# The factor of a normalisation read from a PSUM column instead of SBUF, in a selective-scan layer

## The chip, the cores and the metric

The kernel runs on one core of one Trainium2 chip. The metric is the device time of the whole program in microseconds (us). Engines are called PE (TensorE), DVE or VectorE, ACT or ScalarE, POOL or GpSimd, and SP (the queue that issues most DMAs).

## The reference

Four layers follow each other, each with a residual: `x = x + layer(group_norm(x))`. Only layer 0 is touched here. It is a two-dimensional selective scan over 4 images of 64 x 64 positions and 128 channels, with an inner width of 256:

```
xz = x @ in_proj_w.T ; xh, z = split(xz) ; z = silu(z)
xc = silu(depthwise_conv3x3(xh) + conv_b)
xs = 4 scans of xc: by rows, by columns, and both reversed
h  = exp(delta * A) * h + (delta * u) * B      # along 4096 positions, 16 states per channel
y  = sum over states of h * C, + D * u ; the four directions are summed
mu = y.mean(-1) ; var = y.var(-1)              # over the 256 inner channels of one position
y  = (y - mu) / sqrt(var + EPS) * out_norm_w + out_norm_b
out = (y * z) @ out_proj_w.T
```

The inner norm, `(y - mu) / sqrt(var + EPS)`, is what the change touches. Layers 1 to 3 (a Fourier layer, a layer of spectral convolutions with attention, a neighbourhood attention) come afterwards.

## The kernel before

**The main loop of layer 0.** Work is cut into 128 units: 4 images x 4 directions x 8 chunks of 512 positions (`units`, `per` = 32 units to an image). A unit has 16 slots (`NS`), one for each state number n. A slot does the following, for both halves s of the 256 channels: POOL makes `dB` = du x B (L476, one instruction of 128 x 1024), ACT makes `dA` = exp(delta x A) into a PSUM bank (L482; three banks, pool `psx`), and DVE runs the scan `h` (L483). PE then transposes the finished `h` of an earlier slot (L370, one buffer `pt` of two banks), ACT copies the result to SBUF (L380), and PE contracts over the states (L405). The inputs of the next unit (`inputs`: xd_ps, dp, delta, du) are made in slots 6 to 13 of the current one.

**Side work.** Two generators are woven into the slots. `before` prepares the next image (group norm, in projection, convolution), `after` finishes the previous image (inner norm, gate, out projection, residual). `after` of image b runs during the units of image b + 1; that of the last image has no units left to lie beside and is run in one go at the end (`d.finish(flush_all)`), the drain. Image 0 has no `after` beside it, and the last image no `before`.

`after` works by chunks of 512 positions, held as 4 groups q of 128 positions on the partitions with the 256 channels along the free axis. Means and variances are aggregated once per image into `mv`, and `rs` = 1/sqrt(var + eps) is a tile of 128 x 32 in SBUF. For each chunk: load `y` (called yf in the profile) and `z` (zf); normalise yf in place, four DVE instructions (L256); transpose it on PE into the bank `pg` (L264); scale and shift on ACT into `yg`; multiply with zf on POOL (L270); project on PE into the bank `op` (L275); add the residual on DVE (L281) and store.

**What sets the order.** The order on PE, ACT, DVE and POOL is the one in which the program is written out (`tc.manual_schedule`). The generators stop at `yield` with the kind of step that comes next: "l" a load, "f" a free step, "m" a step that needs the PSUM bank, "z" and "c" matmuls of `before`. At the end of each slot the loop lets at most one step through that needs the bank, `before` ahead of `after`, and only where `free` holds: not in slots 6 to 10 (`BUSY`), not while a convolution is under way, and not before slot `taken`. Steps "f" and "l" go through as soon as they are due. `Side(pieces, count, first, slots)` paces a generator: `count` steps are spread over `slots` slots. `later(place, f, ...)` puts an instruction off to a following slot: "dve" ones are written ahead of that slot's scans, "act0", "act1" and "act2" between its ACT instructions. A call through it stands at line L437 in the profile.

**The bank.** `spare(name)` takes a tile from the pool `psm`, which has a single PSUM bank (tag "m"). In the loop xd_ps, dp, all PSUM tiles of `before`, and pg and op of `after` go through this one bank. The buffers of yf and zf come from a ring of four that the accumulators `y` of the units also use (tag "t4").

Of the kernel before, what the change touches and what calls it, by code (L numbers as in the profile page):

```python
# [12 lines left out]
ALU = mybir.AluOpType  # L13
# [3 lines left out]
P = 128  # L17
# [9 lines left out]
NS = 16  # L27
# [55 lines left out]
def layer0(sh, A, x_in, x_out, scr):  # L83
# [6 lines left out]
    tc, nc = sh.tc, sh.nc  # L90
    with ExitStack() as ctx:
# [144 lines left out]
        def after(b, st, later):  # L236

            mv = small.tile([P, NJ, 2], F32, name="ln_mv")
            for j in range(NJ):
                if j % 8 == 0:  # L240
                    yield "f"
                nc.vector.bn_aggr(mv[:, j, :], st[:, j])
            rs = sh.rstd(small, mv[:, :, 1], [P, NJ], "ln_r")
            exp_and_ln()
            for c in range(NCH):
                yield "l"
                rows = slice(c * CH, (c + 1) * CH)
                y = tmp.tile([P, 4, 2 * P], F32, name="yf", tag="t4", bufs=4)
                nc.sync.dma_start(y, tiles(scr(f"y2{b % 2}")[rows, :]))
                z = tmp.tile([P, 2, CH], F32, name="zf", tag="t4", bufs=4)  # L250
                nc.sync.dma_start(z, scr(f"z{b % 3}")[:, :, rows].rearrange("s p t -> p s t"))
                for q in range(4):
                    if q % 2 == 0:
                        yield "f"
                    j = 4 * c + q
                    nc.vector.tensor_scalar(  # L256
                        y[:, q, :], y[:, q, :], mv[:, j, 0:1], rs[:, j : j + 1], ALU.subtract, ALU.mult
                    )
                yg = tmp.tile([P, 2, CH], F32, name="yg", bufs=1)
                for s in range(2):  # L260
                    yield "m"
                    pt = spare("pg")
                    for q in range(4):
                        nc.tensor.transpose(pt[:, q * P : (q + 1) * P], y[:, q, s * P : (s + 1) * P], sh.ident)  # L264
                    norm = dict(scale=on_w[:, s : s + 1], bias=on_b[:, s : s + 1])
                    later("act0", nc.scalar.activation, yg[:, s, :], pt, AF.Identity, **norm)
                yield "f"
                xr = tmp.tile([P, 4, DM], F32, name="xr", tag="t2", bufs=4)
                nc.sync.dma_start(xr, tiles(x_in(b)[rows, :]))
                nc.gpsimd.tensor_tensor(yg, yg, z, ALU.mult)  # L270
                yield "m"
                op = spare("op").rearrange("p (q d) -> p q d", q=4)
                for q in range(4):
                    for s in range(2):
                        nc.tensor.matmul(  # L275
                            op[:, q, :], lhsT=yg[:, s, q * P : (q + 1) * P], rhs=w_out[:, s, :], start=(s == 0), stop=(s == 1)
                        )
                later("dve", residual, b, rows, xr, op)

        def residual(b, rows, xr, op):  # L280
            nc.vector.tensor_tensor(xr, xr, op, ALU.add)  # L281
            nc.sync.dma_start(tiles(x_out(b)[rows, :]), xr)
# [51 lines left out]
        spare = lambda name: psm.tile([P, CH], F32, name=name, tag="m")  # L334
# [94 lines left out]
        sides = []  # L429
        taken = 0  # L430
        BUSY = range(6, 11)
        todo = {}
        slot = 0

        def later(place, f, *a, slots=1, **kw):

            todo.setdefault((slot + slots, place), []).append(lambda: f(*a, **kw))  # L437

        def flush(place, at=None):
            for f in todo.pop((slot if at is None else at, place), ()):  # L440
                f()
# [6 lines left out]
        with tc.manual_schedule(engines=order):  # L448
            for i, (b, k, c) in enumerate(units):
                if i % per == 0:  # L450
                    ln_st = small.tile([P, NJ, 1, 6], F32, name="ln_st")
# [12 lines left out]
                for n in range(NS):  # L464
                    slot = NS * i + n
                    g, q = divmod(n, 4)
                    if q == 0:
                        B_now = Bb
                        if g < 3:
                            Bb = broadcast(bd, g + 1)  # L470
                        elif i + 1 < len(units):
                            Bb = broadcast(bd_next, 0)
                        h = tmp.tile([P, 2, CH, 4], F32, name="h", bufs=3)
                        G = dict(unit=unit, g=g, h=h, q=0)
                    dB = tmp.tile([P, 2, CH], F32, name="dB", bufs=3)
                    nc.gpsimd.tensor_tensor(dB, du, B_now[:, q : q + 1, :].to_broadcast([P, 2, CH]), ALU.mult)  # L476
                    flush("dve")
                    if i + 1 < len(units) and n in (9, 11):
                        next(coming)
                    for s in range(2):  # L480
                        dA = psx.tile([P, CH], F32, name="dA", tag="x")
                        nc.scalar.activation(dA, delta[:, s, :], AF.Exp, scale=A_neg[:, k, s, n : n + 1])  # L482
                        nc.vector.tensor_tensor_scan(  # L483
                            h[:, s, :, q], dA, dB[:, s, :], state[:, s, n : n + 1], ALU.mult, ALU.add
                        )
                        if s == 0 and i + 1 < len(units):
                            if n in (7, 8, 10):
                                next(coming)
                        elif n == 7 and i + 1 < len(units):
                            bd_next, Wd_next = next(coming)  # L490
                        flush(f"act{s}")
                    copy = transposed() if slot >= LAG else (lambda: None)
                    copy()
                    flush("act2")
                    if q == 2:
                        W = Ws[g] = tmp.tile([P, 32, 16], F32, name="W", bufs=4)
                        nc.sync.dma_start(W, Wd[g, 0 : P * CH].rearrange("(p t a) -> p t a", p=P, a=16))
                    if q == 3:
                        queue.append(G)
                        if c < NCH - 1:  # L500
                            later("act1", nc.scalar.copy, state[:, :, 4 * g : 4 * g + 4], h[:, :, CH - 1, :], slots=5)

                    if i + 1 < len(units):
                        if n == 1:
                            u_next, v_next = fetch(*units[i + 1])
                        if n == 6:
                            coming = inputs(*units[i + 1][1:], v_next, (i + 1) % 2)
                        if n in (6, 7, 9):
                            next(coming)
                        if n == 13:  # L510
                            ready = next(coming)

                    if n == 10:
                        y = unit["y"] = tmp.tile([P, 4, 2 * P], F32, name="y", tag="t4", bufs=4)
                        if k == 0:
                            src = scr("y3").rearrange("(w q r) d -> r w q d", w=64, r=2)
                            for r in range(2):
                                nc.sync.dma_start(y[64 * r : 64 * r + 64], src[r, :, 4 * c : 4 * c + 4, :])
                        elif k != 1:
                            nc.sync.dma_start(y, dst(1 if k == 3 else 0))  # L520

                    inside = [d for d in sides if d.inside]
                    free = n not in BUSY and not inside and slot >= taken
                    able = dict(f=False, l=False, m=free, z=free and n != 5, c=free and n == 11)
                    for d in inside or [d for d in sides if able[d.need] and d.due(slot)][:1]:
                        taken = slot + dict(m=1, z=2, c=3)[d.need]
                        d.free_at = slot + 1
                        d.step()
                    for d in sides:
                        if d.need in ("f", "l") and d.due(slot):  # L530
                            if d.need == "l":
                                d.free_at = slot + 3
                            d.step()
                    sides = [d for d in sides if d.need]
                if i + 1 < len(units):
                    u, bd, Wd = u_next, bd_next, Wd_next
                if i % per == per - 1:
                    slot += 1
                    for d in sides:
                        d.finish(flush_all)  # L540
                    sides = [Side(after(b, ln_st, later), 4 + 8 * 7, NS * (i + 1) + 8, 28 * NS)]
            while queue or copied:
                transposed()()
            for d in sides:
# [1269 lines left out]
```

## Time and profile before

| | |
|---|---|
| median of 3 runs | 8517.93 us (8517.77 to 8523.15) |
| profiled execution | 8527.0 us |
| layer 0's loop of 2048 slots | from 255 to 6143 us |
| drain of layer 0 | to about 6257 us |
| layers 1 to 3 | the rest, about 2270 us |
| busy over the span | DVE 81%, PE 78%, ACT 74%, POOL 64% |

A line of a group reads: line of the program, engine, operation, output <- inputs, shapes, count | busy us in all, mean ns of one | idle us of the engine just before them, and who ended the most of it. A line of the timeline reads: start, length, engine, line, operation, with the idle time ahead of it in brackets. Neighbouring instructions of one group are drawn together in a timeline (x2, x4).

### The profile page before, as it was taken

To read this page: it belongs to the slowest core of one execution; us is meant where nothing else is said; L and a number is where in the kernel's file an instruction comes from. 1 tells how busy PE (TensorE), PEld (TensorE's weight loads), DVE (VectorE), ACT (ScalarE), POOL (GpSimd) and SP (SyncE) were. 2 spreads that over 40 slices of the span, in tenths; PEclk is the share of its full clock that TensorE was granted. 3 is DMA by queue.
4 is the path that set the end of the run, shared out by engine and by line. 5 is a ranking of instruction groups with operands and counts; after the bars stand their busy time and mean duration, and the time that the engine had idled before them with its cause. 6 is when DMAs were issued, how large, how long until landed. Compare 5 with 4: busy or idle time off the path is not lost. (4 is left out here: it accounts for less than half of the span.)

```text
span 8527.0 us, 140477 instructions
## 1 busy us (share of the span) xinstructions
PE 6643.2 (78%) x52976; PEld 4210.6 (49%) x52976; DVE 6867.5 (81%) x7956; ACT 6352.6 (74%) x10268; POOL 5488.4 (64%) x2502
## 2 busy tenths in 40 slices
PE   7688888777788777878877777777668978586689
PEld 3344454444445444444544444444457766464456
DVE  2689999998999999899999999999835454646578
ACT  6799999988988898898888988988812222414467
POOL 0689988988888898888888899999700011020133
PEclk9799999999999999999999999999979989798799
DMA  5445555445555544455554445444341032230332
GB/s 109 137 148 167 171 169 167 167 149 153 181 158 171 169 162 154 154 167 173 169 172 162 153 145 180 166 165 171 132 112 49 23 91 68 81 102 28 91 94 79
DMA packets 1281978, 1163.78 MB, mean 136 GB/s; under 512 B 637974, under 2 KB 1075826, under 8 KB 1214355
## 3 DMA queue, kind: packets, MB, share of 16 engines
q1 hardware_dynamic: 1279618, 1153.06, 42.7%
q8 instruction: 417, 6.83, 0.3%
q14 instruction: 263, 2.15, 0.1%
q10 hardware_dynamic: 1680, 1.74, 0.1%
HBM read 962.66 MB, written 189.74 MB: 135 GB/s over the span
## 5 line engine op out<-in xcount | busy, mean ns | idle before, releaser
L476 POOL TENSOR_TENSOR dB<-du,Bb 128x1024 f32<-128x1024 f32 x2048 | 4821.2, 2385 | 677.6 <-DVE h L483 500.7
L483 DVE TENSOR_TENSOR_SCAN h<-dA,state,dB 128x512 f32<-128x512 f32 x4096 | 4957.1, 1270 | 372.7 <-ACT dA L482 274.3
L370 PE MATMUL pt<-ident,h 128*128 128x128 f32 x16384 | 2268.5, 283 | 1071.8 <-ACT hT L380 1065.6
L482 ACT ACTIVATE dA<-delta,A_neg 128x512 f32<-128x512 f32 x4096 | 2756.3, 693 | 206.3 <-DVE h L483 184.4
L370 PEld LDWEIGHTS pt<-ident,h 128*128 128x128 f32 x16384 | 1854.7, 143 | 2123.0 <-ACT hT L380 1866.6
L380 ACT COPY hT<-pt 128x1024 f32<-128x1024 f32 x2048 | 2072.1, 1012 | 192.5 <-PE pt L370 178.8
L405 PE MATMUL yT<-hT,W 128*32 128x256 f32 x16384 | 1403.1, 415 | 3.1 <-DVE y L421 2.6
L862 POOL COPY XG<-Xs 64x9 f32<-64x9 f32 (+2 forms) x44 | 10.9, 293 | 1028.9 <-DVE in_st L862 675.8
L206 PE MATMUL cv<-xn,taps 128*128 128x512 f32 x1152 | 622.9, 642 | 17.3 <-DVE e L222 8.8
L405 PEld LDWEIGHTS yT<-hT,W 128*32 128x32 f32 x16384 | 454.0, 150 | 355.9 <-issue 341.6
L1535 POOL TENSOR_TENSOR S<-S,sm 128x784 f32<-128x784 f32 x128 | 191.3, 1494 | 406.5 <-DVE sm L1533 342.2
L316 PE MATMUL dp<-xd,w_dt 65*128 65x512 f32 x512 | 299.0, 667 | 127.4 <-ACT Ct L303 91.0
L325 POOL TENSOR_TENSOR du<-delta,u 128x1024 f32<-128x1024 f32 x128 | 305.1, 2384 | 81.8 <-DVE delta L322 81.8
L206 PEld LDWEIGHTS cv<-xn,taps 128*128 128x128 f32 x1152 | 186.3, 191 | 259.2 <-issue 243.5
L297 PE MATMUL xd_ps<-u,w_x 128*48 128x512 f32 x512 | 256.9, 626 | 46.2 <-DMA u<-l_xw 19.5
L1542 ACT ACTIVATE S<-S,mx 128x196 f32<-128x196 f32 x512 | 229.1, 451 | 33.9 <-DVE mx L1569 33.4
L316 PEld LDWEIGHTS dp<-xd,w_dt 65*128 65x128 f32 x512 | 79.2, 195 | 242.4 <-ACT Ct L303 149.0
L672 ACT ACTIVATE h<-pf,b 128x512 f32<-128x512 f32 x128 | 88.2, 689 | 146.5 <-PE pf L671 146.5
L322 DVE SCALAR_TENSOR_TENSOR delta<-delta,dp 128x512 f32<-128x512 f32 x256 | 169.5, 662 | 28.4 <-ACT delta L320 28.4
L319 ACT ACTIVATE delta<-dp 128x512 f32<-128x512 f32 x256 | 152.8, 597 | 52.7 <-PE dp L316 48.7
L1411 POOL MEMSET kp<- 128x210 f32 (+1 forms) x8 | 1.8, 285 | 275.2 <-DMA x<-m 275.2
L256 DVE TENSOR_SCALAR yf<-yf,ln_mv,ln_r 128x256 f32<-128x256 f32 x128 | 169.2, 1368 | 3.2 <-DMA yf<-l_y 3.2
(334 smaller groups left out, 7444.9 us busy)
## 6 DMA issues: line engine op xcount, KB each, us to landing
Bb<-l_B SPq DMA_DIRECT2D x512, 1024.0 KB
W<-l_W SPq DMA_DIRECT2D x512, 256.0 KB
l_y<-y SPq DMA_DIRECT2D x128, 512.0 KB
u<-l_xw SPq DMA_DIRECT2D x64, 512.0 KB
y<-l_y SPq DMA_DIRECT2D x64, 512.0 KB
u<-l_xr SPq DMA_DIRECT2D x64, 512.0 KB
V<-l_v SPq DMA_DIRECT2D x512, 49.0 KB
wr<-wt SPq DMA_DIRECT2D x128, 136.0 KB
```

The source lines that it names most:

```text
L206: nc.tensor.matmul(pm, lhsT=taps[:, s, t, :], rhs=xn[:, dy : dy + 8, dx : dx + 64], start=(t == 0), stop=(t == 8),)
L297: nc.tensor.matmul(xd_ps, lhsT=w_x[:, s, k, :], rhs=u[:, s, :], start=(s == 0), stop=(s == 1))
L316: nc.tensor.matmul(dp, lhsT=w_dt[:, k, s * P : (s + 1) * P], rhs=xd, start=True, stop=True)
L325: nc.gpsimd.tensor_tensor(du, delta, u, ALU.mult)
L370: nc.tensor.transpose(pt[:, j, s, :], G["h"][:, s, t0 : t0 + 32, :].rearrange("p t n -> p (t n)"), sh.ident)
L380: return lambda: nc.scalar.copy(hT, pt.rearrange("p j s d -> p j (s d)"))
L405: nc.tensor.matmul(U["yT"][e][32 * jo : 32 * jo + 32, qo % 2, :], lhsT=U["Ws"][G["g"]][:, :, 4 * q + j], rhs=hT[:, j, :], start=((e, jo) n ...
L476: nc.gpsimd.tensor_tensor(dB, du, B_now[:, q : q + 1, :].to_broadcast([P, 2, CH]), ALU.mult)
L482: nc.scalar.activation(dA, delta[:, s, :], AF.Exp, scale=A_neg[:, k, s, n : n + 1])
L483: nc.vector.tensor_tensor_scan(h[:, s, :, q], dA, dB[:, s, :], state[:, s, n : n + 1], ALU.mult, ALU.add)
L1535: nc.gpsimd.tensor_tensor(Sv, Sv, U["sm"].unsqueeze(2).to_broadcast([P, 4, 196]), ALU.mult)
L1542: nc.scalar.activation(Sn, Sn, AF.Exp, bias=U["mx"][:, n : n + 1], accum_out=sm[:, n : n + 1])
```

## The change

The four normalising instructions of a chunk become `scalar_tensor_tensor`: the mean is still a per-partition scalar from SBUF, but the factor is now a second tensor operand, a PSUM column spread over the 256 elements with a stride of zero. ACT copies the chunk's four columns of `rs` into the bank first (`nb`). The chunk's two "f" steps become one step "n" that needs the bank, may not fall into slot 5, and keeps it for two slots; its four instructions are put off to the following slot with `later`. The number of steps of `after` is given as 52 instead of 60.

```diff
                 z = tmp.tile([P, 2, CH], F32, name="zf", tag="t4", bufs=4)
                 nc.sync.dma_start(z, scr(f"z{b % 3}")[:, :, rows].rearrange("s p t -> p s t"))
+                yield "n"
+
+                nb = spare("nb")[:, 0:4]
+                nc.scalar.copy(nb, rs[:, 4 * c : 4 * c + 4])
                 for q in range(4):
-                    if q % 2 == 0:
-                        yield "f"
-                    j = 4 * c + q
-                    nc.vector.tensor_scalar(
-                        y[:, q, :], y[:, q, :], mv[:, j, 0:1], rs[:, j : j + 1], ALU.subtract, ALU.mult
-                    )
+                    later("dve", normed, y[:, q, :], mv[:, 4 * c + q, 0:1], nb[:, q : q + 1])
...
+        def normed(y, mean, factor):
+            nc.vector.scalar_tensor_tensor(y, y, mean, factor.to_broadcast([P, 2 * P]), ALU.subtract, ALU.mult)
...
-                    able = dict(f=False, l=False, m=free, z=free and n != 5, c=free and n == 11)
+                    able = dict(f=False, l=False, m=free, n=free and n != 5, z=free and n != 5, c=free and n == 11)
                     for d in inside or [d for d in sides if able[d.need] and d.due(slot)][:1]:
-                        taken = slot + dict(m=1, z=2, c=3)[d.need]
+                        taken = slot + dict(m=1, n=2, z=2, c=3)[d.need]
...
-                    sides = [Side(after(b, ln_st, later), 4 + 8 * 7, NS * (i + 1) + 8, 28 * NS)]
+                    sides = [Side(after(b, ln_st, later), 4 + 8 * 6, NS * (i + 1) + 8, 28 * NS)]
```

## The prediction

> **What bounds the kernel now.** I read the page's table of groups first, then the stage by stage table of busy time cut at the starts of the four images of layer 0, then the groups of VectorE alone in the stretch where the changed line runs, then its waits, and last the timeline around single instructions of the line and in the drain after the last scan.
>
> The groups of the page show the loop of layer 0 and the line that is changed:
>
> ```profile
> L476 POOL TENSOR_TENSOR dB<-du,Bb 128x1024 f32<-128x1024 f32 x2048 | 4821.2, 2385 | 677.6 <-DVE h L483 500.7
> L483 DVE TENSOR_TENSOR_SCAN h<-dA,state,dB 128x512 f32<-128x512 f32 x4096 | 4957.1, 1270 | 372.7 <-ACT dA L482 274.3
> L482 ACT ACTIVATE dA<-delta,A_neg 128x512 f32<-128x512 f32 x4096 | 2756.3, 693 | 206.3 <-DVE h L483 184.4
> L256 DVE TENSOR_SCALAR yf<-yf,ln_mv,ln_r 128x256 f32<-128x256 f32 x128 | 169.2, 1368 | 3.2 <-DMA yf<-l_y 3.2
> ```
>
> To see there: POOL's longest idle time is ended by VectorE's scan, and VectorE's own idle time is only 373 us over the whole loop. The changed line takes 1368 ns for 256 elements, though a scan over 512 takes 1270.
>
> The table by image (stretches of 512 slots each; columns are the length, then PE, weight load, DVE, ACT, POOL busy, with instruction counts in brackets):
>
> ```profile
> 255.10:1711.30 1456.20, 1172.04 (x8870) 680.50 (x8870) 1341.89 (x1225) 1338.21 (x1976) 1279.35 (x559) 0.97 0.49 161
> 1711.30:3220.70 1509.40, 1198.28 (x9170) 704.94 (x9170) 1399.06 (x1305) 1342.63 (x1991) 1299.29 (x567) 0.98 0.51 164
> 3220.70:4735.70 1515.00, 1205.84 (x9170) 709.11 (x9170) 1401.14 (x1305) 1342.60 (x1991) 1299.05 (x567) 0.97 0.50 163
> 4735.70:6142.70 1407.00, 1047.64 (x8760) 638.90 (x8760) 1356.41 (x1240) 1268.13 (x1868) 1290.40 (x553) 0.97 0.46 161
> ```
>
> VectorE is busy 92 to 96% of each, more than any other engine. Its idle time is 114, 110, 114 and 51 us. The first image carries no `after` side work and yet idles as long as the next two: what VectorE does more there, the stretch is longer by. So I take VectorE as the engine whose work sets the length of a stretch.
>
> Its groups from 1711.3 to 6142.7 us:
>
> ```profile
> L256 DVE TENSOR_SCALAR yf<-yf,ln_mv,ln_r 128x256 f32<-128x256 f32 x96 | 158.1, 1688 | 0.0
> L322 DVE SCALAR_TENSOR_TENSOR delta<-delta,dp 128x512 f32<-128x512 f32 x190 | 125.8, 662 | 0.0
> L222 DVE SCALAR_TENSOR_TENSOR e<-cv,cols,e 128x512 f32<-128x512 f32 x32 | 23.7, 740 | 0.0
> L437 DVE TENSOR_SCALAR xn<-x_ps,gn_s,gn_o 128x320 f32<-128x320 f32 x26 | 15.3, 589 | 0.0
> L437 DVE TENSOR_SCALAR xn<-x_ps,gn_s,gn_o 128x384 f32<-128x384 f32 x2 | 1.3, 655 | 0.0
> ```
>
> Of the 128 instructions of L256, 96 lie beside the scans, at 1688 ns; the last 32 lie in the drain. All rows with an operand in PSUM are near their size (662 to 740 ns for 512). Why L256 is long shows the timeline:
>
> ```profile
> 2008.71 4.74 POOL L476 TENSOR_TENSOR dB<-du,Bb 128x1024 f32<-128x1024 f32 x2 [0.23 <-DVE h L483]
> 2010.82 2.78 DVE L256 TENSOR_SCALAR yf<-yf,ln_mv,ln_r 128x256 f32<-128x256 f32 x2
> 2013.52 2.45 DVE L483 TENSOR_TENSOR_SCAN h<-dA,state,dB 128x512 f32<-128x512 f32 x2
> ```
>
> The pair begins at 2010.82 and ends at 2013.60, just after POOL's second product ends (2013.45). In the drain, where POOL is silent, four of them take 1.38 us (below). So some 2.4 us of a pair are a wait for POOL to finish.
>
> [...] 0.38 us at the least against 2.465 at the most for L256, and none of the listed rows with a PSUM operand shows such a tail. [...]
>
> **The change part by part**, against the profile's own span of 8527.0 us (the three other runs: 8517.8 to 8523.2, 0.1% lower; I subtract from their median).
>
> 1. Removed: 96 tensor_scalar beside the loop, 158.1 us of VectorE. The wait inside them is on the path: nothing of VectorE's runs beside it, and the scans are queued behind.
>
> 2. Added in their place: 96 scalar_tensor_tensor of 256 elements, one operand in PSUM, one per-partition scalar in SBUF. Nearest rows: 740 ns (with such a scalar) and 662 (without), for 512. One element costs (655 - 589)/64 = 1.03 ns, so 256 fewer take off 265: 475 or 397 ns. Back to back, instructions overlap a little at the ends (the residual sum of 0.69 us starts 0.61 before its successor in the drain), some 0.07 each. Four take 1.3 us at the least, 1.9 at the most; I take 1.65. 24 chunks: 40 us. VectorE saves 158 - 40 = 118 us.
>
> 3. Added: one ScalarE copy of 128x4 into PSUM per chunk. Nearest row is the state copy of 128x8, 0.186 us. 24 x 0.19 = 5 us of ScalarE, queued ahead of the next dA. ScalarE idles over 100 us in each image, so this could hide; I charge it whole, 5 us. Bounds 0 and, if the copy waits for the bank at each chunk, 24 x 1.2 = 29 us (half a slot each; a slot is 2.87 us).
>
> 4. The bank: nb takes the single bank tagged "m" until the fourth product. The step is kept out of slots 5 to 10, where xd_ps and dp use it, and `taken` keeps other side steps off for two slots. In the two built programs' orders the whole of `before` stands in the same slots as it did, and all eight chunks of an image still end inside it (the last residual in unit 29 of 32, formerly 28). Cost nothing beyond 3; it is hidden by the gap of side steps.
>
> 5. Moved: yf and zf loads issue up to 52 slots later on SP's queue, past Bb, W and y loads, the xr load and the x store with them; the pg transposes and yg activations move by up to 50 slots, and so does the POOL product. Numbers and bytes stay. In the loop no instruction waited visibly for a yf load (the only 3.2 us is in the drain), and zf and yf buffers are held 15 to 66 slots, formerly 27 to 68. Nothing on average; plus or minus 10 us for collisions that differ.
>
> 6. The drain after the last scan has all of chunk 0 to 7 of the last image in a row:
>
> ```profile
> 6210.65 0.69 DVE L281 TENSOR_TENSOR xr<-xr,op 128x512 f32<-128x512 f32 x1 [9.59 <-PE op L275]
> 6211.26 1.38 DVE L256 TENSOR_SCALAR yf<-yf,ln_mv,ln_r 128x256 f32<-128x256 f32 x4
> 6211.73 1.13 PEld L264 LDWEIGHTS pg<-ident,yf 128*128 128x128 f32 x4 [1.42 <-issue]
> 6213.26 0.78 ACT L437 ACTIVATE yg<-pg,cols 128x512 f32<-128x512 f32 x1 [8.95 <-PE pg L264]
> 6214.09 1.12 PE L264 MATMUL pg<-ident,yf 128*128 128x128 f32 x4 [0.93 <-ACT yg L437]
> ```
>
> From the residual sum's start to the first yg it is now 2.61 us, with the transposes running one behind each product. Afterwards nb needs the bank that the residual sum reads: 0.69 + 0.04 to the copy, 0.19 copy, 0.04, four products 1.65, and only then is the bank free for pg: 0.09, transposes 1.12, 0.1: 3.9 us. So +1.3 for each of seven chunks, and +1.0 for the first, whose copy hides behind the yf load: +10 us, all on the path. Bounds 7 and 14.
>
> Sum: -118 + 5 + 10 = -103 against 8527; 8518 - 103 = 8415.
>
> A cross-check by slots (from one slot's first scan to the next one's, in the timeline): the 48 slots that carry a pair of L256 last 5.8 us on average, where slots with the same other VectorE work and no L256 last about 3 us less; 48 x 3 = 143, less 40 and with the drain, gives -93. Against the first image (1456 us, with a start-up of about 15), images two and three would come to 1456 - 15 + 21 of remaining `after` work on VectorE (13 products, 5 residual, 3 aggregates) = 1462, 50 less than now; over three images with 40 for the last, -140 + 10 = -130. I stay between, with the VectorE sum.
>
> **The rivals.** (a) Freed VectorE time turns partly into idle time, since ScalarE at 1343 us and POOL at 1299 an image are close behind: the scan already waits 177 us on dA and 67 on dB from 1711 us on. Against it: the first image runs with ScalarE at the same 1338 us in 1456. If half of the 118 goes so: -59 + 15 = -44, 8474. (b) More than the sum: POOL (365 us ended by h) and ScalarE (166 us) waited through the same stalls, and a loop without them idles less. The comparison with image one gives -130, 8388; at the extreme 8365. (c) The change doesn't do what it says: the new product still blocks behind POOL, through its SBUF side. Then four products take about what two pairs took, 24 x 6.6 = 158 again, and only 15 us come on top: 8533, within the uncertain band. The rows of 662 to 740 ns speak against it; break-even lies at (158 - 15)/96 = 1.49 us per product. (d) Slower: ScalarE's in-order queue stops at the nb copy until VectorE has released the bank, and every dA behind it, and so every scan, waits. It decides from 103/24 = 4.3 us of loss per chunk; at 6 us (two slots) 24 x 6 - 103 = +41, 8559. For it: ScalarE now loses 84 us to xd_ps, which goes through that bank, up to 3.5 at once. Against: ScalarE is not two slots ahead of VectorE, since dA has three banks, and the bank's last reader is at least one slot back.
>
> **How the numbers follow.** A difference of 0.2%, 17 us, is about what a measurement of this kernel can tell from none. Chances: the sum as worked out, from -75 to -130 us, 0.66 (its own range 8388 to 8443); (a) 0.14; (b) 0.12; (c) 0.03; (d) 0.05. Until no more than two in ten is left out, the range takes half of (a) and half of (b): 8372 to 8468. Faster: 0.66 + 0.14 + 0.12 = 0.92; same 0.03; slower 0.05.
>
> **What would show it.** VectorE's row of yf in the loop at 0.40 to 0.47 us each with no tail near 2.4, and the four in 1.3 to 1.9 us (step 2); images two and three near 1470 us with VectorE idle still near 110 (step 1, against (a)); an nb copy of about 0.2 us with little idle ahead of it, and no long dA wait behind it (step 3, 4, against (d)); the drain's period per chunk near 12.8 us instead of 11.5 (step 6); layers 1 to 3 as long as before. Wrong it would be if yf stays over 1 us, if VectorE's idle time grows by tens of us an image, or if the bank stops ScalarE.

## The result, and the profile after

The changed kernel takes 8418.92 us (median of 4 runs, 8411.85 to 8426.25) against 8520.54 us before (4 runs): a ratio of 0.9881, 95% interval 0.9864 to 0.9898, so 1.0 to 1.4% faster. The forecast was 8415.

The page's groups of the loop, of the changed kernel (its line numbers are two higher from the loop on):

```profile
span 8415.0 us, 140563 instructions
...
L485 DVE TENSOR_TENSOR_SCAN h<-dA,state,dB 128x512 f32<-128x512 f32 x4096 | 4956.1, 1269 | 370.7 <-ACT dA L484 280.0
L478 POOL TENSOR_TENSOR dB<-du,Bb 128x1024 f32<-128x1024 f32 x2048 | 4816.7, 2386 | 563.7 <-DVE h L485 421.9
...
L484 ACT ACTIVATE dA<-delta,A_neg 128x512 f32<-128x512 f32 x4096 | 2747.5, 690 | 138.0 <-DVE h L485 113.0
```

The scans and their own idle time are as they were (371 us against 373). What fell is the time for which POOL and ScalarE waited for a scan: POOL from 501 to 422 us, ScalarE from 184 to 113.

VectorE's new row in the loop, and ScalarE's copy (groups of one engine each):

```profile
L280 DVE SCALAR_TENSOR_TENSOR yf<-yf,ln_mv,nb 128x256 f32<-128x256 f32 x96 | 39.2, 470 | 0.0
```
```profile
L255 ACT COPY nb<-ln_r 128x4 f32<-128x4 f32 x24 | 4.2, 174 | 0.0
```

The lengths of all 128 normalising instructions, those of the drain included, as shortest/median/longest in ns, before and after:

```profile
L256 DVE TENSOR_SCALAR yf<-yf,ln_mv,ln_r x128: 381/907/2465, 1850.8 to 6246.5; 128x256 f32<-128x256 f32 x128
L280 DVE SCALAR_TENSOR_TENSOR yf<-yf,ln_mv,nb x128: 454/474/482, 1984.6 to 6137.1; 128x256 f32<-128x256 f32 x128
```

Where 96 instructions took 158.1 us, they now take 39.2, and the longest of all 128 is 0.482 us instead of 2.465. The copies cost ScalarE 4.2 us in all, and VectorE never sat idle for one of them beside the scans.

The table of the four images (length, then PE, weight load, DVE, ACT, POOL busy):

```profile
251.90:1709.30 1457.40, 1173.22 (x8870) 681.44 (x8870) 1342.38 (x1224) 1335.72 (x1976) 1279.33 (x560) 0.96 0.49 161
1709.30:3191.70 1482.40, 1195.49 (x9172) 705.50 (x9170) 1365.47 (x1305) 1339.92 (x1999) 1297.94 (x567) 0.98 0.51 167
3191.70:4669.60 1477.90, 1190.34 (x9170) 702.59 (x9170) 1364.77 (x1305) 1339.62 (x1999) 1297.69 (x567) 0.98 0.51 167
4669.60:6023.60 1354.00, 1026.06 (x8760) 626.47 (x8760) 1310.30 (x1240) 1266.14 (x1876) 1288.16 (x553) 0.99 0.47 167
```

The first image, which carries no `after` work, is what it was (1457 against 1456 us). The other three are 27, 37 and 53 us shorter, and VectorE's busy time in them is 34, 36 and 46 us lower. Its idle time there is 117, 113 and 44 us, formerly 110, 114 and 51.

One chunk of the drain (timeline):

```profile
6109.06 0.69 DVE L283 TENSOR_TENSOR xr<-xr,op 128x512 f32<-128x512 f32 x1 [10.40 <-PE op L274]
6109.83 0.17 ACT L255 COPY nb<-ln_r 128x4 f32<-128x4 f32 x1 [7.12 <-DVE xr L283]
6110.03 1.66 DVE L280 SCALAR_TENSOR_TENSOR yf<-yf,ln_mv,nb 128x256 f32<-128x256 f32 x4 [0.29 <-ACT nb L255]
6112.98 0.78 ACT L439 ACTIVATE yg<-pg,cols 128x512 f32<-128x512 f32 x1 [2.98 <-PE pg L263]
...
6122.10 0.69 DVE L283 TENSOR_TENSOR xr<-xr,op 128x512 f32<-128x512 f32 x1 [10.41 <-PE op L274]
```

The copy stands in wait for the residual sum to free the bank, the products for the copy, and yg starts 3.92 us after the residual sum where it started 2.61 us after it. A chunk's period is 12.9 us (11.5 before).

Added up for the two profiled executions: loop 5887.6 to 5771.7 us, -115.9; from the end of the last scan to the start of the last residual sum 114.0 to 123.9, +9.9; start-up 255.1 to 251.9 and everything after layer 0 2270.4 to 2267.4, -6.2 together. These two scatter by as much among the other kernels below (249 to 254 us, 2263 to 2271), so nothing is read from them. The sum is -112.2 (the spans differ by 112.0, the rest is rounding); the medians differ by 101.6, since each profile shows one run only.

### The profile page after: what moved, and what is told of

It is laid out like the page before. It is cut to its first block, busy times and chain, and to the rows that moved or that the text cites. A ratio compares the mean times of both kernels' runs of the same rounds, so it can differ in the third digit from the quotient of the medians.

```text
span 8415.0 us, 140563 instructions
## 1 busy us (share of the span) xinstructions
PE 6597.0 (78%) x52976; PEld 4189.2 (50%) x52976; DVE 6753.7 (80%) x7956; ACT 6340.7 (75%) x10300; POOL 5482.8 (65%) x2502
## 5 line engine op out<-in xcount | busy, mean ns | idle before, releaser
L269 POOL TENSOR_TENSOR yg<-yg,zf 128x1024 f32<-128x1024 f32 x32 | 75.7, 2367 | 145.9 <-ACT yg L439 131.2
```

## The experiments

All edits are against the changed kernel unless it says otherwise. The kernel before took 8520.7 to 8521.7 us beside them.

**The operand alone.**

```diff
-                    later("dve", normed, y[:, q, :], mv[:, 4 * c + q, 0:1], nb[:, q : q + 1])
+                    later("dve", normed, y[:, q, :], mv[:, 4 * c + q, 0:1], rs[:, 4 * c + q : 4 * c + q + 1])
...
-            nc.vector.scalar_tensor_tensor(y, y, mean, factor.to_broadcast([P, 2 * P]), ALU.subtract, ALU.mult)
+            nc.vector.tensor_scalar(y, y, mean, factor, ALU.subtract, ALU.mult)
```

> The changed kernel with its order, its step n, its copy nb and its hold on the bank, but with the four instructions of a chunk as tensor_scalar again, the factor from SBUF (nb is copied and read by nobody). [...] the operand alone is the cause, so the 96 instructions in the loop wait for POOL again. One after the other, the first of a chunk meets a POOL product at a random point of its 2.4 us and the rest may each meet the next: between 1.2 + 3 x 0.35 = 2.3 us and 4 x 2.4 = 9.6 us a chunk, where the change has 1.65; about 5.5 as in the two pairs of the kernel before gives 24 x 3.9 = +94 us in the loop, and the drain is shorter by about 9 us since pg no longer waits for the products to free the bank: about 8505, anywhere from 8430 to 8540. Order (rival): the gain came from grouping and spacing the steps anew, so about 8410 (8419 less the 9 of the drain).

Measured: 8495.04 us, ratio to before 0.9966 (0.9953 to 0.9979). Its row in the loop and one of its groups of four in the timeline:

```profile
L280 DVE TENSOR_SCALAR yf<-yf,ln_mv,ln_r 128x256 f32<-128x256 f32 x96 | 111.7, 1222 | 0.0
```
```profile
1982.65 2.36 POOL L327 TENSOR_TENSOR du<-delta,u 128x1024 f32<-128x1024 f32 x1
1983.03 5.14 DVE L280 TENSOR_SCALAR yf<-yf,ln_mv,ln_r 128x256 f32<-128x256 f32 x4
1984.97 2.41 POOL L478 TENSOR_TENSOR dB<-du,Bb 128x1024 f32<-128x1024 f32 x1
1988.09 4.80 DVE L485 TENSOR_TENSOR_SCAN h<-dA,state,dB 128x512 f32<-128x512 f32 x4
```

The order, the copy and the hold on the bank are all in place, and yet 76 of the 102 us between the medians come back with the operand. In the loop it is 91 of 116 us, while the drain falls back to 113.6 us. The remaining 25 us of the loop go with the new order: the kernel before has 64 of its 96 instructions over 1 us, this one only 40. The lines show how one group of four goes. The first two of four wait out du and dB; then POOL stops for 3.31 us (its next product starts at 1990.68, released by a scan), and the other two run free at 0.40 us. Two pairs in two slots, as before the change, can meet a running POOL twice: both pairs waited in 23 of the 24 chunks there.

**The new operation without PSUM.**

```diff
-                nb = spare("nb")[:, 0:4]
-                nc.scalar.copy(nb, rs[:, 4 * c : 4 * c + 4])
...
-                    later("dve", normed, y[:, q, :], mv[:, 4 * c + q, 0:1], nb[:, q : q + 1])
+                    later("dve", normed, y[:, q, :], mv[:, 4 * c + q, 0:1], rs[:, 4 * c + q : 4 * c + q + 1])
```

> The changed kernel without the copy nb: the new instruction (scalar_tensor_tensor), but with the factor's column spread from SBUF, so two SBUF inputs. [...] each product waits for POOL as before, yf at 1.2 to 2.4 us on average, loop +60 to +170 us, drain -9: 8470 to 8580. Rival ([...] it was the change of operation that helped): yf stays at 0.46 us, 8410, and PSUM was not needed.

Measured: 8516.56 us, ratio 0.9995 (0.9987 to 1.0004): all of the gain is gone.

```profile
L278 DVE SCALAR_TENSOR_TENSOR yf<-yf,ln_mv,ln_r 128x256 f32<-128x256 f32 x96 | 121.7, 1325 | 0.0
```
```profile
L278 DVE SCALAR_TENSOR_TENSOR yf<-yf,ln_mv,ln_r x128: 458/478/4482, 1985.3 to 6235.5; 128x256 f32<-128x256 f32 x128
```

The same instruction takes 1325 ns in the mean with both tensors in SBUF and 470 with one of them in PSUM. So the rival falls: it is the PSUM operand that helps, not the operation. Of the 96, 43 are longer than 1 us, and most of these end 0.28 us after a POOL instruction.

Its drain takes 116.9 us, with the new operation but neither the copy nor the bank. That is used below.

**The accumulator written out, all in SBUF.** Against the kernel before, with its order:

```diff
-                        y[:, q, :], y[:, q, :], mv[:, j, 0:1], rs[:, j : j + 1], ALU.subtract, ALU.mult
+                        y[:, q, :], y[:, q, :], mv[:, j, 0:1], rs[:, j : j + 1], ALU.subtract, ALU.mult, accum_out=rows_sum
```

> The kernel before with its order, its steps f and its SBUF factor, but with tensor_scalar also writing out its accumulator (to a spare column). [...] no wait for POOL although every operand lies in SBUF; [...] 4 x 0.5 = 2.0 us a chunk, loop -158 + 48 = -110, drain +0 to +5 us: 8410 to 8425, as good as the change without bank or copy. Rival (it is the SBUF operands[...]): waits stay, 8520.

That this form would not wait, and its 0.5 us an instruction, were estimates of the author's that no trace had shown. The kernel leaves the factor out of yf; it prices the instruction only. Measured: 8408.61 us, ratio 0.9866 (0.9849 to 0.9882).

```profile
L257 DVE TENSOR_SCALAR_CACHE_REDUCE yf<-yf,ln_mv,ln_r 128x256 f32<-128x256 f32 x96 | 50.6, 527 | 1.8
L257 DVE DVE_READ_ACCUMULATOR yf<-yf,ln_mv,ln_r 128x1 f32 x96 | 7.9, 82 | 0.0
```
```profile
L257 DVE TENSOR_SCALAR_CACHE_REDUCE yf<-yf,ln_mv,ln_r x128: 509/538/542, 1846.2 to 6132.0; 128x256 f32<-128x256 f32 x128
```

No instruction waits for POOL (the longest is 0.542 us), though its operands lie in SBUF, and its loop is as long as that of the change (5767 against 5772 us) with the old order and no bank. Together the three runs say: the gain of the loop comes from taking VectorE's wait for POOL away, by PSUM or by the form, and order adds little once nothing waits. What inside the chip makes VectorE wait is not shown; the runs show only on which operands and forms the wait depends. The drain missed the expectation: it takes 122.1 us, 8 more than before where at most 5 were expected, and most of that is the length of the form: four take 2.29 us there where tensor_scalar takes 1.38.

**POOL's product in halves.** Against the kernel before:

```diff
-                    nc.gpsimd.tensor_tensor(dB, du, B_now[:, q : q + 1, :].to_broadcast([P, 2, CH]), ALU.mult)
+                    for s in range(2):
+                        nc.gpsimd.tensor_tensor(dB[:, s, :], du[:, s, :], B_now[:, q, :], ALU.mult)
```

> The kernel before with POOL's product dB cut in two instructions of 128x512 each in place of one of 128x1024. [...] a tensor_scalar waits for the POOL instruction that is running and no longer, so L256's longest falls from 2.46 us to about 1.3 (half of 2.38, and 0.1), still ending 0.15 us after a POOL instruction's end; the mean of the 96 in the loop falls from 1.69 to about 1 us, -50 us or more on L256. The whole need not be faster, since POOL pays a start for each of 2048 more instructions: if that is 0.1 us, POOL goes from 2.38 to 2.48 a slot and may become the bound, 8480 to 8750. Rival (the wait is for the slot's other work, for a buffer or for ScalarE): L256's longest stays near 2.46.

Measured: 8505.14 us, ratio 0.9983 (0.9976 to 0.9989), and a miss on the row: the longest L256 rose to 6.69 us and the mean in the loop stayed at 1.72.

```profile
1999.36 7.47 POOL L477 TENSOR_TENSOR dB<-du,Bb 128x512 f32<-128x512 f32 x6
1999.83 2.44 DVE L484 TENSOR_TENSOR_SCAN h<-dA,state,dB 128x512 f32<-128x512 f32 x2
2002.18 5.12 DVE L256 TENSOR_SCALAR yf<-yf,ln_mv,ln_r 128x256 f32<-128x256 f32 x2
```

Of 60 instructions over 0.8 us, 41 waited for one POOL instruction (up to 1.39 us, the half that was expected); the other 19 waited through 3 to 5 in a row and came in when POOL's train of products ended (2006.83; the first of the pair above ends at 2006.98). The lengths of all 128 (shortest/median/longest):

```profile
L256 DVE TENSOR_SCALAR yf<-yf,ln_mv,ln_r x128: 382/478/6691, 1845.9 to 6216.6; 128x256 f32<-128x256 f32 x128
```

So a wait ends with the end of a POOL instruction, as in all 64 cases before (0.15 us after it), but not always with that of the first. The rival (a buffer, or ScalarE) has nothing for it. All 19 long waits ended where POOL itself stopped for 2.9 us or more; all of the 41 short ones ended while POOL went straight on. With whole products it is rare but not absent: in the run with both tensors in SBUF, one instruction of 4.48 us waited out the rest of one product and the whole of the next, and went in when POOL stopped. Why an instruction is passed over at all is open.

The loop is 26 us shorter than before (5861 us) although VectorE is busy 16 us longer and POOL runs two products of 1.29 us for one of 2.39: VectorE's idle time fell from 389 to 347 us, that for dA from 177 to 124 in the three later images. So idle time is not a constant of this loop.

**The drain.**

```diff
+                if b == NB - 1:
+                    for q in range(4):
+                        j = 4 * c + q
+                        nc.vector.tensor_scalar(
+                            y[:, q, :], y[:, q, :], mv[:, j, 0:1], rs[:, j : j + 1], ALU.subtract, ALU.mult
+                        )
+                else:
+                    ...  # as in the change
```

> The changed kernel, but the last image, whose after work is all in the drain where POOL has next to nothing to do, is normalised as before: tensor_scalar with the factor from SBUF, no copy nb, no hold on the bank. Theory (the drain pays 1.3 us a chunk for nb and for transposes that wait until the fourth product has freed the bank): the drain's period per chunk falls from 12.9 back to 11.5 us, -10 us in all, 8409 where the change has 8419, with the loop as it is. Rival (the longer drain comes from something else, such as PE's clock there): period stays near 12.9, 8419.

Measured: 8403.93 us, ratio 0.9861 (0.9847 to 0.9876). The loop is as in the change (5770.3 us), the drain is back at 113.3 us with a period of 11.48, from 123.9 and 12.89. So the ten microseconds come from the new way of normalising, and not from PE's clock there (granted 0.64 before, 0.62 with the change). They are not all the bank's: the run with both tensors in SBUF uses the new operation (four in 1.67 us where tensor_scalar takes 1.38) without the copy and the bank, and its drain takes 116.9 us. About 3 of the ten are the slower operation, 7 the copy and the hold on the bank. Two chunks follow each other like this:

```profile
6067.12 0.69 DVE L289 TENSOR_TENSOR xr<-xr,op 128x512 f32<-128x512 f32 x1 [8.98 <-PE op L280]
6067.72 1.37 DVE L255 TENSOR_SCALAR yf<-yf,ln_mv,ln_r 128x256 f32<-128x256 f32 x4
...
6078.69 0.69 DVE L289 TENSOR_TENSOR xr<-xr,op 128x512 f32<-128x512 f32 x1 [9.59 <-PE op L280]
```

**Less and more of VectorE.** The first leaves the products and the copy out of three images, the second adds four products per chunk into a spare tile, the third adds four instructions that don't touch the bank.

The three edits in one, with notes behind the #:

```diff
+                if b == NB - 1:                       # less: copy and products stand under this
+                    nb = spare("nb")[:, 0:4]
...
+                if b < NB - 1:                        # more, both kernels
+                    for q in range(4):
+                        later("dve", spared, spare_out, y[:, q, :], mv[:, 4 * c + q, 0:1], nb[:, q : q + 1])
...
+            nc.vector.scalar_tensor_tensor(out, y, mean, factor.to_broadcast([P, 2 * P]), ALU.subtract, ALU.mult)   # spared, from the bank
...
+            nc.vector.tensor_scalar(out, y, mean, 0.0, ALU.subtract, ALU.add, accum_out=spare_sum)   # spared, off the bank
```

> The changed kernel with the normalising products and the copy nb left out for the three images whose after work lies beside the scans (their yf goes on unnormalised); the drain is left whole. If the loop's length follows VectorE's busy time: 24 x 1.55 = -37 us, 8382, VectorE idle per image staying near 115 us. If other engines hold the loop now (ScalarE, POOL): less than -15 us, above 8404, with VectorE's idle time up by what is taken away.

> The changed kernel with four more products per chunk, into a spare tile that nobody reads, for the three images in the loop; 96 more instructions of 0.39 us from start to start, 24 x 1.55 = 37 us of VectorE. If the loop's length follows VectorE's busy time one to one: 8456. If only the two thirds that leaving the products out gave back (22 of 37): 8443. If other engines hide it: below 8430. ScalarE has nothing added; the bank is held 1.55 us longer per chunk.

> The changed kernel with four more instructions per chunk in the loop, as in the run with the work doubled, but they don't read the bank: tensor_scalar with its accumulator written out, from yf into a spare tile, that showed no wait for POOL. About 4 x 0.5 = 2.0 us of VectorE per chunk, queued in the same place. If the doubled run's +66 us in the loop came from a longer stall of VectorE as such: again +60 to +70, 8479. If from the bank's longer hold (PE's xd_ps, dp, pg behind it): +37 to +45, 8460.

Measured: 8397.3 us (0.9854, 0.9839 to 0.9869), 8479.22 (0.9951, 0.9934 to 0.9967) and 8479.36 (0.9951, 0.9938 to 0.9965). The tables of the second and third image, less first, then more:

```profile
1708.70:3179.40 1470.70, 1193.93 (x9170) 704.99 (x9170) 1352.73 (x1273) 1339.21 (x1991) 1298.01 (x567) 0.98 0.53 169
3179.40:4651.30 1471.90, 1198.67 (x9170) 706.59 (x9170) 1353.19 (x1273) 1339.23 (x1991) 1297.73 (x567) 0.98 0.52 168
```
```profile
1707.20:3207.80 1500.60, 1204.62 (x9170) 711.10 (x9170) 1380.39 (x1337) 1340.31 (x1999) 1297.46 (x567) 0.97 0.52 165
3207.80:4712.30 1504.50, 1216.24 (x9170) 717.80 (x9170) 1380.20 (x1337) 1340.30 (x1999) 1297.80 (x567) 0.96 0.51 165
```

Against the change, over all four images:

| | VectorE busy, us | loop, us |
|---|---|---|
| products left out | -37 | -28 |
| four more, from the bank | +47 | +66 |
| four more, off the bank | +46 | +62 |
| tensor_scalar again | +75 | +91 |
| the kernel before | +116 | +116 |

For the first two, neither plain expectation holds in these profiles (the third came out as its first branch, 8479, said): the loop follows VectorE's work, but 0.8 for one on the way down and 1.3 to 1.4 on the way up. Each row is one profile, while the runs of one kernel spread over 9 to 18 us. The medians, -22, +60 and +60 us against the change, go the same way; the intervals, 12 to 14 us either way for each kernel, leave one for one possible. Part of the miss on the way up was the size: the extra instructions all write one tile and take some 0.48 us of VectorE each, where the change's start 0.39 us after each other. A longer hold of the bank is out as a cause, since the third kernel does without it.

A slot with the four products lasts 3.91 us, with eight 5.85: 1.94 us more for 1.94 us of work. Over 24 slots that is 47 of the 66 us, so the whole of the added work reaches its slot. The other 19 us are idle time of VectorE, nearly all of it ahead of scans that wait for dA (the change, then four more from the bank, from 1700 to 6000 us):

```profile
L485 DVE TENSOR_TENSOR_SCAN h<-dA,state,dB 128x512 f32<-128x512 f32 x3063 | 3702.9, 1269 | 256.8 <-ACT dA L484 180.7 <-POOL dB L478 63.8 <-issue 0.9
L492 DVE TENSOR_TENSOR_SCAN h<-dA,state,dB 128x512 f32<-128x512 f32 x3008 | 3640.2, 1269 | 276.5 <-ACT dA L491 201.5 <-POOL dB L485 61.3 <-issue 2.2
```

Why dA came later there was not traced.

**Two lumps instead of one.** Against the version with the direct drain:

```diff
-                        later("dve", normed, y[:, q, :], mv[:, 4 * c + q, 0:1], nb[:, q : q + 1])
+                        later("dve", normed, y[:, q, :], mv[:, 4 * c + q, 0:1], nb[:, q : q + 1], slots=1 + q // 2)
...
-                    able = dict(f=False, l=False, m=free, n=free and n != 5, z=free and n != 5, c=free and n == 11)
+                    able = dict(f=False, l=False, m=free, n=free and n not in (4, 5), z=free and n != 5, c=free and n == 11)
...
-                        taken = slot + dict(m=1, n=2, z=2, c=3)[d.need]
+                        taken = slot + dict(m=1, n=3, z=2, c=3)[d.need]
```

> The version with the direct drain (8404), and the four products of a chunk in the loop put two into one slot and two into the next, with the bank kept a slot longer and step n kept out of slot 4 too. Leaving the products out gave back 28 us of the loop, 1.2 us for a lump of 1.65; four more took 66, 2.75 us for 1.95 more. If a lump's cost grows faster than its length, because dA has three banks and dB three buffers of lead that a short stall uses up only in part: two lumps of 0.8 cost some 0.4 each, -9 us, 8395. If it is VectorE's sum that counts: 8404, no change. If the longer hold of the bank costs more: above 8410.

Measured: 8395.77 us (5 runs), ratio 0.9850 (0.9837 to 0.9864), the fastest version here that computes everything. Its median is 8 us below the direct drain's, as expected, but the intervals overlap (0.9847 to 0.9876 there), and of the loop's 6 us gain (5770 to 5764) the second and third image have 13 while the last lost 6. That the smaller lumps are the cause is not shown.

## Why the prediction was right

- **VectorE sets the length of a stretch, and its idle time stays.** Right for this change: -115.6 us of busy time went with -115.9 us of loop, and idle time stayed within 7 us per image. As a rule it is rougher than it looked: putting tensor_scalar back gave 91 us of loop for 75 of work, the runs with less and more work point off one to one too, and with POOL's product in halves idle time fell by 42 us. That it came out so near one to one here may be partly luck.
- **The wait for POOL (step 1).** Right in what it depends on, and shown three ways: with the operand put back 1222 ns in the mean, with a second SBUF input 1325, with the accumulator written out 527 and no wait. What the trace had for a PSUM operand were the rows with one: before the change the 256 instructions delta<-delta,dp took 653 to 689 ns each. The size of the wait was put at some 2.4 us a pair; the 48 pairs took 3.29 us on average where the one free pair took 0.71, so 2.6. The sum doesn't use it.
- **The product (step 2).** Four in 1.63 to 1.66 us, taken at 1.65; 470 ns each, near the upper of the two ends (475), that of the row with a per-partition scalar.
- **The copy (step 3).** 0.174 us, near the 0.186 of the row it was taken from, but charged 5 us in full where VectorE lost nothing visible to it. The loop came out at -116 where the steps gave -113. A slip without effect: half of a slot of 2.87 us is 1.4 us, not 1.2, so the upper bound was some 34 us rather than 29.
- **The bank and the moved steps (steps 4, 5).** PE's transposes of h waited behind nb 7 times in the whole program, 6.6 us together; VectorE never did in the loop. Rival (d) fell.
- **The drain (step 6).** 3.92 us to the first yg against 3.9 worked out, +9.9 us against +10; the direct drain takes it away again.
- **The rivals.** (c), that the new product still blocks, would have been right with the factor in SBUF: 8517 us, no gain. (a) and (b) are not needed for this change: VectorE's idle time over the loop was 389 us before and after, though POOL's wait for the scans did fall as (b) said. The cross-check against the first image, on which (b) rests, was too good: it gave 1462 us for images two and three, which took 1482 and 1478.

## What to carry to other kernels

When a VectorE row has a minimum near its size and a maximum near the length of a GpSimd instruction (here 0.381 and 2.465 us, beside GpSimd's 2.39), compare its ends with GpSimd's: here the wait inside the row showed as busy time (158.1 us, with 0.0 idle ahead of it) and in no list of waits. Moving one operand to PSUM took it out for 0.17 us of ScalarE per chunk. In the drain, where GpSimd is nearly silent (busy 18.7 of 114.3 us before), the old form was the better one by ten microseconds, since the new operation is slower there (four in 1.67 us against 1.38) and the copy and the shared bank stand in the chain (about 7 of the ten). Price the new form by the row with the same kind of operands (with a per-partition scalar 740 ns for 512 elements, without one 662). Let the loop's gain be the change of busy time only if idle time is seen not to depend on it.

## What the runs showed that was not expected

- A VectorE instruction that waits for GpSimd can be passed over by several GpSimd instructions: with products of 1.29 us, 19 of 60 waited through 3 to 5 of them, up to 6.69 us; with products of 2.39 us, all 64 of the kernel before waited for exactly one, but one of 43 with two SBUF inputs waited through two. Shorter GpSimd instructions did not make the waits shorter on average (1.72 us in the mean against 1.69).
- The end of a wait has its own delay by form: waiting tensor_scalar instructions end 0.15 us after GpSimd's, most scalar_tensor_tensor with two SBUF inputs 0.28 us after.
- tensor_scalar with its accumulator written out takes 527 + 82 ns for 256 elements and waits for nothing (0.542 us at the most), in a loop where the plain form took 1688 ns in the mean.
